# Softplus in one ScalarE instruction, one transposition of dt·x, and eleven to twelve pre-added states in a selective-scan network

## Chip, cores and metric

One core of a Trainium2 chip runs the whole program. The metric is the device time of one execution in microseconds (us); lower is better. Engines are named as the profile names them: PE (TensorE, matmuls), PEld (its weight loads), DVE (VectorE), ACT (ScalarE), POOL (GpSimd) and SP (SyncE, which issues the DMAs).

## The reference

Eight images of 192 channels and 64x64 positions pass through four layers. Layers 0 and 2 hold a selective scan over the 4096 positions in four directions. For each direction, channel and state n of 16:

```python
dt = softplus(einsum('kcr,bkrl->bkcl', dt_proj_w, dts) + dt_proj_b)
h  = h * exp(dt_t[..., None] * A) + (dt_t * x_t)[..., None] * B_t[:, :, None, :]
y  = einsum('bkcn,bkn->bkc', h, C_t)
```

Layer 1 uses a softplus too, but no recurrence: `gain = sum_k(bc * softplus(dtr @ dt_w + dt_b) + D)`, between two layer norms, SiLU gates and 1x1 projections. Layer 3 is a windowed attention-like block made of small convolutions. All is float32.

## The kernel before

**The order of the program.** For each image: `scan_layer` (layer 0), `layer0_out` and `layer1`, `put_sequences`, `scan_layer` again (layer 2), and `between` (the rest of this image together with the start of the next one). So `scan_layer` runs 16 times.

**The scan.** A scan layer has 48 units, `k`. A unit is one pass `d` (forward or backward) over one chunk of 512 positions for one third `v` of the work: v=0 and v=1 are 128 channels of one pair of directions each, v=2 holds the 64 left-over channels of both. The three units v=0, 1, 2 of a chunk follow each other. A unit has eight sub-blocks `j` of 64 positions, and the order of the instructions is written out by hand in one loop over k and j (lines 348 to 398); the scheduler is told to keep it (`tc.manual_schedule()`, line 93). In iteration j each engine gets its part of several units at once, and each engine works through its own queue in order:

- DVE: `scan(k, j)` (lines 286 to 301): two operations of 16 elements that carry the state over (lines 294 and 296), then the scan over 16 states x 64 positions (line 299). At j=2 `finish(k-2)` (line 332 or 336), at j=4 `steps_b(k+2)` (line 220), at j=6 and 7 of v=1 and v=2 the building of the diagonals (line 193).
- PE: `fill(k, j+1)` (line 281) computes the scan's input `u` in PSUM from 32-row slices of the transposed dt·x; `u` has two buffers, so the fill for scan j+1 waits for scan j-1. Then `turn(k+1)` (line 234) at j=2, `steps_a(k+2)` (lines 208 and 210) at j=3, the projection of the next chunk at j=4 and 5 of v=0 (lines 141 to 151), diagonals at j=5 (line 183), and `add_up` (line 324), which sums states over n with an identity matrix.
- ACT: at j=2 the copies of the transposed dt·x out of PSUM (line 236), then the 16 decays `exp(dt·a)` of the next unit (line 244) in groups given by the table DECAY; at j=4 the softplus of unit k+2 (`steps_l`, lines 215 to 217): Abs, Exp and Ln, whose result DVE turns into `max(z,0)+ln(1+exp(-|z|))` (line 220); at j=7 `cut(k+1)` (lines 253 and 254), which saves and clears the first column of the decays.
- POOL: the product with C (line 311), the pre-addition of states 12 to 15 to states 8 to 11 (line 312), and dt·x at j=5 (lines 225 and 226).

Small PSUM results (projection, dt before softplus, transpositions, diagonals) share the tag `misc`, which has two buffers, used in turn.

**Two arrangements.** A fill uses rows (positions) in blocks of 32. `windows()` (line 169) gives two arrangements r=0 and r=1 of the chunk, the second shifted by 64 positions; dt·x is transposed in both (eight transpositions per unit), and is extended by 64 positions for it (line 226).

**Outside the scan.** The other phases are ordered by a list scheduler. An activation function needs its table in ACT; `preload_act_table_set` loads one by hand, and the compiler adds loads where a function is not in the table that is there. In `layer1`, four steps `u` normalise (line 651), make three projections with SiLU (line 657), and then loop four times over the directions with the softplus (lines 670 to 698).

Of the kernel before, what the change touches and what calls it, by code (L numbers as in the profile page):

```python
# [40 lines left out]
def tile_net(ctx: ExitStack, tc: tile.TileContext, a: dict, out: bass.AP):  # L41
# [39 lines left out]
    def scan_layer(pk, wx, wd):  # L81
# [2 lines left out]

        table = tc.keep_in_program_order(nc.scalar.preload_act_table_set(EXP_LN))
        with (
            tc.tile_pool(name="sc_c", bufs=1) as sc,
            tc.tile_pool(name="sc_w", bufs=2) as sw,  # L90
# [11 lines left out]
            nc.sync.dma_start(out=msk, in_=a["msk"])  # L102

            neg_a = sc.tile([P, 3, 2, NS], F32, name="neg_a")
            with tc.issue_after(table.ins):
                nc.scalar.activation(neg_a, par[:, :, :, 0:NS], AF.Exp)
            nc.vector.tensor_scalar_mul(neg_a, neg_a, -1.0)
            skip = sc.tile([P, 3], F32, name="skip")
            nc.vector.tensor_tensor(skip, par[:, :, 0, 17], par[:, :, 1, 17], ALU.add)
# [1 line left out]
            carry = [sc.tile([P, NS], F32, name=f"carry{v}") for v in range(3)]  # L111

            nck = T // Q
            NP = 12
            units = [
                (d, i, i if d == 0 else nck - 1 - i, v)
# [49 lines left out]

            def windows():
                for r in range(2):  # L170
                    for w in range(NSUB // 4):
                        for e in range(2):
                            t0 = r * SB + w * 4 * SB + e
                            yield (r * 2 + w) * 2 + e, slice(t0, t0 + 2 * P - 1, 2)
# [34 lines left out]
                else:  # L209
                    nc.tensor.matmul(pz, wdt[:, d, 1, :], x, start=True, stop=True)  # L210

            def steps_l(k):

                t = dts[k] = sw.tile([P, Q], F32, tag="dt", name="dt")
                nc.scalar.activation(t, pzs[k], AF.Abs)
                nc.scalar.activation(t, t, AF.Exp, scale=-1.0)
                nc.scalar.activation(t, t, AF.Ln, bias=one)  # L217

            def steps_b(k):
                nc.vector.scalar_tensor_tensor(dts[k], pzs.pop(k), 0.0, dts[k], ALU.max, ALU.add)  # L220

            def steps_c(k):
                x = vt[k // 3][:, units[k][3], :]
                dtx[k] = sw.tile([P, Q + SB], F32, tag="dtx", name="dtx")
                nc.gpsimd.tensor_tensor(dtx[k][:, 0:Q], dts[k], x, ALU.mult)  # L225
                nc.gpsimd.tensor_tensor(dtx[k][:, Q : Q + SB], dts[k][:, 0:SB], x[:, 0:SB], ALU.mult)

            def turn(k):

                dtt[k] = sw.tile([P, NSUB, P], F32, tag="dtt", name="dtt")  # L230
                for i, cols in windows():
                    if i % 4 == 0:
                        pt = misc()
                    nc.tensor.transpose(pt[:, i % 4 * P : (i % 4 + 1) * P], dtx[k][:, cols], ident)  # L234
                    if i % 4 == 3:
                        nc.scalar.copy(dtt[k][:, i - 3 : i + 1].rearrange("p i c -> p (i c)"), pt)  # L236

            def decay(k, n0, n1):

# [29 lines left out]
            def fill(k, j):  # L269

                d, i, c, v = units[k]
                s = j if d == 0 else NSUB - 1 - j
                u = us[k, j] = sp.tile([P, NS, SB], F32, tag="u", name="u", bufs=2)
                for e in range(2):
                    for r in range(2):
                        w, q = divmod((s - r) % NSUB, 4)
                        i = (r * 2 + w) * 2 + e
                        rows = slice(q * 32, (q + 1) * 32)
                        for o in ((v,) if v < 2 else (0, 1)):
                            ch = slice(0, P) if v < 2 else slice(o * CB, (o + 1) * CB)  # L280
                            nc.tensor.matmul(  # L281
                                u[ch, r * 8 : r * 8 + 8, e:SB:2], dtt[k][rows, i, ch],
                                dg[k // 3, o][rows, i], start=True, stop=True,
                            )

# [22 lines left out]
            def times_c(k, g):  # L308
                s = 2 * g if units[k][0] == 0 else NSUB - 2 - 2 * g
                h = das[k][:, s : s + 2]  # L310
                nc.gpsimd.tensor_tensor(h, h, cts.pop((k, g)), ALU.mult)  # L311
                nc.gpsimd.tensor_tensor(h[:, :, 8:NP], h[:, :, 8:NP], h[:, :, NP:NS], ALU.add)  # L312

            def load_y(k):
                d, i, c, v = units[k]
# [4 lines left out]
            def add_up(k, n0, n1):  # L320
                if n0 == 0:
                    py[k] = sp.tile([P, Q], F32, tag="py", name="py")
                for n in range(n0, n1):
                    nc.tensor.matmul(  # L324
                        py[k], ident, das[k][:, :, n, :], start=(n == 0), stop=(n == NP - 1)
                    )

            def finish(k):
# [16 lines left out]
            def has(k):  # L345
                return 0 <= k < nu

            for k in range(-6, nu + 2):
                m, v = divmod(k, 3)
                ahead = 0 <= m + 1 < nm  # L350
                for j in range(NSUB):
# [20 lines left out]
                    if j == 2:  # L372
# [3 lines left out]
                            load_y(k - 1)  # L376
                        if has(k + 1):
                            turn(k + 1)
                    if j == 3 and has(k + 2):
                        steps_a(k + 2)  # L380
                    if v == 0 and ahead:
                        if j == 4:
                            project_a(m + 1)
# [7 lines left out]
                    kk = k - 1 if j > 2 else k - 2  # L391
                    if has(kk) and j in SUM:
                        add_up(kk, *SUM[j])
                    if j == 4 and has(k + 2):
                        steps_l(k + 2)
                        steps_b(k + 2)
                    if has(k + 1) and j in DECAY:
                        decay(k + 1, *DECAY[j])

# [222 lines left out]
    def layer1(x):  # L622
        with (
# [25 lines left out]
            with tc.issue_after(table.ins):  # L649
                for u in range(NU):  # L650
                    norm(wk, wide_, part(x, u), vec(0), vec(1), part(xn, u), "sq")
            for u in range(NU):
                src = part(xn, u)
                for dst, ww, c0 in ((s2, w, O_X2), (xs, wc, 0), (z, wc, 192)):
                    ps = linear(psum, ww, c0, src)
                    for i in range(2):
                        nc.scalar.activation(part(dst, u)[i], ps[i], AF.Silu)
            table = tc.keep_in_program_order(nc.scalar.preload_act_table_set(EXP_LN))
            with tc.issue_after(table.ins):
                for u in range(NU):  # L660
                    src, gain = part(xs, u), part(xn, u)
# [8 lines left out]
                    for k in range(4):  # L670
                        pk, pz = wide_("pk"), (wide_("pza"), narrow_("pzb"))
                        r = [slice((k - h) % 4 * 32, (k - h) % 4 * 32 + 32) for h in range(2)]
                        for h in range(2):
                            nc.tensor.matmul(
                                pz[0][:, h], wdt[r[h], h, 0:CA], dtr[r[h], h], start=True, stop=True
                            )
                        for h in range(2):
                            nc.tensor.matmul(
                                pz[1][half(h)], wdt[r[h], h, CA:192], dtr[r[h], h], start=True, stop=True
                            )  # L680
                        for h in range(2):
                            nc.tensor.matmul(
                                pk[:, h], sel[r[h], 0:P], bc[r[h], h], start=True, stop=True
                            )
                        sp_ = step_pair(wk, "sp")
                        for i in range(2):
                            nc.scalar.activation(sp_[i], pz[i], AF.Abs)
                            nc.scalar.activation(sp_[i], sp_[i], AF.Exp, scale=-1.0)
                            nc.scalar.activation(sp_[i], sp_[i], AF.Ln, bias=one)
                            nc.vector.scalar_tensor_tensor(  # L690
                                sp_[i], pz[i], 0.0, sp_[i], ALU.max, ALU.add
                            )
                        if k == 0:
                            spread(tt, gain, sp_, pk, ALU.mult)
                        else:
                            spread(tt, sp_, sp_, pk, ALU.mult)
                            for i in range(2):
                                tt(gain[i], gain[i], sp_[i], ALU.add)
                    for i in range(2):
                        nc.vector.scalar_tensor_tensor(  # L700
                            gain[i], gain[i], d_sum[i], src[i], ALU.add, ALU.mult
                        )
                for u in range(NU):
                    y, s, xc = part(xn, u), part(s2, u), part(x, u)
                    norm(wk, wide_, y, vec(2), vec(3), y, "sq")
# [9 lines left out]
    PE_TAPS = 4  # L715


    def behind(b, pool, wk, psp):

        wide_, narrow_ = psp  # L720
        x = new_pair(pool, "x")
# [24 lines left out]
        yt = [t[:, 0:T] for t in yt]  # L746
        for u in range(NU):
            s = join(narrow_, wk, yt, u)
            norm(
                wk, wide_, s, [v[:, 0:1] for v in v2], [v[:, 1:2] for v in v2], part(x, u), "join"  # L750
            )
            yield "norm"

        xc = room("t2", size["t2"])[:, 0:T]
# [182 lines left out]
            yield "out"  # L937


    def ahead(b, pool, wk, psp):  # L940

        wide_, narrow_ = psp
        w0 = load_both(pool, a["w0"], 384, "w0")
# [21 lines left out]
        yield "load"  # L965
        for u in range(NU):
            hu = part(h, u)
            norm(wk, wide_, hu, col["ln_g"], col["ln_b"], hu, "sta")
            yield "norm"
        for u in range(NU):  # L970
            hu = part(h, u)
# [95 lines left out]
    def between(done, todo):  # L1067

        with (
# [2 lines left out]
            ExitStack() as stack,  # L1072
        ):
            gens = []
            alone = done is None or todo is None
            for name, fn, b in (("c", behind, done), ("a", ahead, todo)):
                if b is None:
# [8 lines left out]
                def narrow_(what, name=name):  # L1086
                    return psp.tile([P, Q], F32, tag="pb" + name, name=what + name, bufs=2)

                gens.append(fn(b, pool, wk, (wide_, narrow_)))
            while gens:  # L1090
                for g in list(gens):
                    if next(g, None) is None:
# [136 lines left out]
```

## Time and profile before

| | |
|---|---|
| three timed runs | 28047.61 us median, 28042.4 to 28049.32 |
| profiled execution | 28045.14 us, span 28043.0 us |
| busy share of the span | PE 85%, DVE 78%, POOL 71%, ACT 49% |
| granted TensorE clock, mean | 0.919 |
| image 0, from the trace: first scan layer | about 209 to 1436 us |
| layer 0's end, layer 1 and the sequences | 1436 to 1948 us (with the second scan layer's start) |
| second scan layer | 1948 to 3177 us |
| `between`, to the next image's first scan | 3177 to 3702 us |
| table loads in the trace | 190, of 1.28 us each |

The profile's page gives the busy time of each engine over the whole span, groups of instructions by source line, and waits by who released them. The timeline lists instructions in order: start, duration, engine, line, operation, and in brackets the idle time ahead of it and who ended it. The windows view gives the busy time of each engine in a stretch and the granted TensorE clock there (1.00 is full speed). Since nearly three quarters of the time lies in sixteen scan layers that repeat one pattern every three units, the place to read is one such chunk.

### The profile page before, as it was taken

The numbers are of one execution on the slowest core, as the hardware profiler recorded it, in microseconds if no ns is written. First come the engines' busy times: TensorE is split into PE (matmuls) and PEld (weight loads), VectorE is DVE, ScalarE is ACT, GpSimd is POOL, SyncE is SP. The second block draws the span as 40 slices with busy tenths as digits, with TensorE's granted clock in tenths as the row PEclk, the third lists the DMA queues.
The fourth block names the chain that finished last, engine by engine and source line by source line (L and its number), as shares of the span: only waits on it lengthen the run. The fifth ranks groups of instructions, "written<-read, shape, count | busy, mean of one in ns | idle before, by whom it ended". The sixth has DMA issues, their size and how long they took to land.

```text
span 28043.0 us, 311528 instructions
## 1 busy us (share of the span) xinstructions
PE 23809.1 (85%) x109960; PEld 10557.4 (38%) x109960; DVE 21950.2 (78%) x25269; ACT 13815.8 (49%) x22366; POOL 19824.5 (71%) x8284
## 2 busy tenths in 40 slices
PE   8979879798797987979889798897988979889797
PEld 3424334243342433424334243342433424334243
DVE  7959779597795977959789597895978859788596
ACT  5545445454454544545445454454544545445453
POOL 6929679296792957929579295792957929579296
PEclk9979989799897998979989799897998979989798
DMA  5626556265562655626556265562655626556264
GB/s 153 193 85 188 145 155 194 83 188 145 157 192 83 190 143 158 193 83 189 142 159 192 83 189 142 160 190 86 191 140 160 187 87 190 141 160 188 88 190 130
DMA packets 1239290, 4286.43 MB, mean 153 GB/s; under 512 B 427920, under 2 KB 454384, under 8 KB 839408
## 3 DMA queue, kind: packets, MB, share of 16 engines
q1 hardware_dynamic: 1237744, 4266.51, 51.7%
q8 instruction: 886, 14.52, 0.2%
q14 instruction: 660, 5.41, 0.1%
HBM read 3810.80 MB, written 450.72 MB: 152 GB/s over the span
## 4 chain that ended last, share of the span: by engine, by line
PE 25%; DVE 23%; ACT 11%; issue 4%; POOL 3%; DMA 2%; SPq 0%; DVEq 0%; POOLq 0%; ACTq 0%
DVE da L299 15%; PE u L281 7%; PE py L324 7%; ACT da L244 5%; PE pa L450 2%; DVE dg L193 1%; DVE u L296 1%; POOL da L311 1%; ACT dtt L236 1%; POOL acc L873 1%; PE misc L234 1%; PE pa L453 1%; ACT dt L217 1%; DVE tmp L294 1%; DVE dt L220 1%
## 5 line engine op out<-in xcount | busy, mean ns | idle before, releaser
L311 POOL TENSOR_TENSOR da<-da,ct 128x2048 f32<-128x2048 f32 x3072 | 13929.5, 4534 | 725.0 <-DVE tmp L294 265.2
L299 DVE TENSOR_TENSOR_SCAN da<-da,u 128x1024 f32<-128x1024 f32 x6144 | 14049.4, 2287 | 379.4 <-ACT da L254 91.5
L324 PE MATMUL py<-da,ident 128*128 128x512 f32 x18432 | 9348.1, 624 | 62.4 <-POOL da L311 62.4
L281 PE MATMUL u<-dg,dtt 32*128 32x256 f32 x65536 | 7075.4, 400 | 1706.2 <-DVE da L299 1677.2
L244 ACT ACTIVATE da<-dt,neg_a 128x512 f32<-128x512 f32 x12288 | 7708.4, 710 | 0.0
L281 PEld LDWEIGHTS u<-dg,dtt 32*128 32x128 f32 x65536 | 4163.9, 161 | 6358.2 <-issue 3972.4
L324 PEld LDWEIGHTS py<-da,ident 128*128 128x128 f32 x18432 | 3137.2, 190 | 4071.7 <-issue 3751.3
L225 POOL TENSOR_TENSOR dtx<-dt,vt 128x512 f32<-128x512 f32 x768 | 978.8, 1275 | 4652.9 <-DMA vt<-vs 3888.5
L312 POOL TENSOR_TENSOR da<-da 128x512 f32<-128x512 f32 x3072 | 3901.7, 1270 | 240.9
L236 ACT COPY dtt<-misc 128x512 f32<-128x512 f32 x1536 | 829.8, 589 | 6277.1 <-PE misc L234 6277.1
L296 DVE TENSOR_TENSOR u<-u,tmp 128x16 f32<-128x16 f32 x6048 | 1106.5, 183 | 703.5 <-PE u L281 55.6
L193 DVE TENSOR_TENSOR dg<-msk,misc 128x1024 f32<-128x1024 f32 x1024 | 1223.1, 1197 | 0.0
L220 DVE SCALAR_TENSOR_TENSOR dt<-misc,dt 128x512 f32<-128x512 f32 x768 | 531.3, 692 | 780.5 <-ACT dt L217 624.4
L234 PE MATMUL misc<-ident,dtx 128*128 128x128 f32 x6144 | 980.6, 304 | 62.2 <-POOL dtx L225 51.4
L294 DVE TENSOR_TENSOR tmp<-da,da 128x16 f32<-128x16 f32 x5376 | 937.9, 174 | 119.0
L234 PEld LDWEIGHTS misc<-ident,dtx 128*128 128x128 f32 x6144 | 818.3, 209 | 342.7 <-issue 225.6
L824 POOL MEMSET t<- 128x4356 f32 (+2 forms) x32 | 99.8, 3120 | 1190.5 <-DVE t L798 1031.0
L858 PE MATMUL pwc<-t,l3taps 128*128 128x486 f32 (+1 forms) x1280 | 724.5, 705 | 241.5 <-DVE u L878 143.5
L253 ACT COPY da<-da 128x128 f32<-128x128 f32 x768 | 294.3, 383 | 1096.9 <-DVE tmp L294 1079.4
L875 DVE SCALAR_TENSOR_TENSOR acc<-t,l3p,acc 128x486 f32<-128x486 f32 (+1 forms) x480 | 479.6, 1026 | 415.0 <-POOL acc L873 411.2
L208 PE MATMUL misc<-xd,wdt 64*128 64x512 f32 x1024 | 615.6, 683 | 13.4 <-ACT xd L155 13.4
L141 PE MATMUL misc<-vt,wxt 128*128 128x512 f32 x512 | 318.0, 706 | 362.9 <-DMA vt<-vs 362.9
(289 smaller groups left out, 19493.8 us busy)
## 6 DMA issues: line engine op xcount, KB each, us to landing
ct<-cd SPq DMA_DIRECT2D x2048, 1024.0 KB
ct<-cd SPq DMA_DIRECT2D x2048, 512.0 KB
vt<-vs SPq DMA_DIRECT2D x768, 256.0 KB
yp<-yo SPq DMA_DIRECT2D x384, 256.0 KB
yo<-yp SPq DMA_DIRECT2D x384, 256.0 KB
ys<-yo SPq DMA_DIRECT2D x384, 256.0 KB
yt<-ys SPq DMA_DIRECT2D x96, 512.0 KB
t<-ys SPq DMA_DIRECT2D x96, 512.0 KB
```

What stands on the lines that cost most here:

```text
L193: nc.vector.tensor_tensor(dg[m, o][:, at], msk[:, 0:32].unsqueeze(1).unsqueeze(1).to_broadcast(shape), bts[m, o][:, at, r * 8 : r * 8 + 8] ...
L225: nc.gpsimd.tensor_tensor(dtx[k][:, 0:Q], dts[k], x, ALU.mult)
L234: nc.tensor.transpose(pt[:, i % 4 * P : (i % 4 + 1) * P], dtx[k][:, cols], ident)
L236: nc.scalar.copy(dtt[k][:, i - 3 : i + 1].rearrange("p i c -> p (i c)"), pt)
L244: nc.scalar.activation(das[k][:, :, n, :], dts[k].rearrange("p (s t) -> p s t", t=SB), AF.Exp, scale=neg_a[:, v, d, n : n + 1],)
L281: nc.tensor.matmul(u[ch, r * 8 : r * 8 + 8, e:SB:2], dtt[k][rows, i, ch], dg[k // 3, o][rows, i], start=True, stop=True,)
L294: nc.vector.tensor_tensor(tmp, da0[:, k % 2, s, :], prev, ALU.mult)
L296: nc.vector.tensor_tensor(head, head, tmp, ALU.add)
L299: nc.vector.tensor_tensor_scan(h, h, u.rearrange("p n t -> p (n t)")[:, way], 0.0, ALU.mult, ALU.add)
L311: nc.gpsimd.tensor_tensor(h, h, cts.pop((k, g)), ALU.mult)
L312: nc.gpsimd.tensor_tensor(h[:, :, 8:NP], h[:, :, 8:NP], h[:, :, NP:NS], ALU.add)
L324: nc.tensor.matmul(py[k], ident, das[k][:, :, n, :], start=(n == 0), stop=(n == NP - 1))
```

## The change

1. **Softplus.** In the scan the three ACT instructions and the DVE one become one ACT instruction `Softplus`. Its table does not hold Exp, so the three units of the next chunk are done together, in v=1 at j=3 and j=4, between two table loads; `dt` gets four buffers. In layer 1 the same replacement is made, and the table loads there are placed by hand: norms, SiLU, softplus and the last norms each under one load. In `between` the norms are placed behind one load.
2. **One transposition.** dt·x is transposed once (four transpositions instead of eight). The first arrangement is one ACT copy of the PSUM tile; the second is made by four more ACT copies of 32 partitions x 512 elements each, shifted by 32 partitions. The extension by 64 positions on POOL goes.
3. **Pre-added states.** POOL adds four states for the first two of a unit's four groups, and three for the last two; the state left out is summed by one more PE matmul over half the columns.

```diff
-            def steps_l(k):
-                t = dts[k] = sw.tile([P, Q], F32, tag="dt", name="dt")
-                nc.scalar.activation(t, pzs[k], AF.Abs)
-                nc.scalar.activation(t, t, AF.Exp, scale=-1.0)
-                nc.scalar.activation(t, t, AF.Ln, bias=one)
             def steps_b(k):
-                nc.vector.scalar_tensor_tensor(dts[k], pzs.pop(k), 0.0, dts[k], ALU.max, ALU.add)
+                dts[k] = sw.tile([P, Q], F32, tag="dt", name="dt", bufs=4)
+                nc.scalar.activation(dts[k], pzs.pop(k), AF.Softplus)
             def steps_c(k):
-                dtx[k] = sw.tile([P, Q + SB], F32, tag="dtx", name="dtx")
-                nc.gpsimd.tensor_tensor(dtx[k][:, 0:Q], dts[k], x, ALU.mult)
-                nc.gpsimd.tensor_tensor(dtx[k][:, Q : Q + SB], dts[k][:, 0:SB], x[:, 0:SB], ALU.mult)
+                dtx[k] = sw.tile([P, Q], F32, tag="dtx", name="dtx")
+                nc.gpsimd.tensor_tensor(dtx[k], dts[k], vt[k // 3][:, units[k][3], :], ALU.mult)
             def turn(k):
-                for i, cols in windows():
-                    if i % 4 == 0:
-                        pt = misc()
-                    nc.tensor.transpose(pt[:, i % 4 * P : (i % 4 + 1) * P], dtx[k][:, cols], ident)
-                    if i % 4 == 3:
-                        nc.scalar.copy(dtt[k][:, i - 3 : i + 1].rearrange("p i c -> p (i c)"), pt)
+                pt = misc()
+                for i, cols in windows(1):
+                    nc.tensor.transpose(pt[:, i * P : (i + 1) * P], dtx[k][:, cols], ident)
+                pt = pt.rearrange("p (w x) -> p w x", w=2)
+                nc.scalar.copy(dtt[k][:, 0], pt)
+                for q in range(4):
+                    src = pt[(q + 1) % 4 * 32 : (q + 1) % 4 * 32 + 32]
+                    nc.scalar.copy(dtt[k][q * 32 : q * 32 + 32, 1], src if q < 3 else src[:, ::-1])
             def times_c(k, g):
-                nc.gpsimd.tensor_tensor(h[:, :, 8:NP], h[:, :, 8:NP], h[:, :, NP:NS], ALU.add)
+                n = NS - NP if g < 2 else NS - NP - 1
+                to = h[:, :, NP - n : NP]
+                nc.gpsimd.tensor_tensor(to, to, h[:, :, NS - n : NS], ALU.add)
             def add_up(k, n0, n1):
+                if n0 < NP // 2 <= n1:
+                    s = slice(0, NSUB // 2) if units[k][0] else slice(NSUB // 2, NSUB)
+                    nc.tensor.matmul(py[k][:, s.start * SB : s.stop * SB], ident,
+                        das[k][:, s, NP, :], start=False, stop=False)
...
-                    if j == 3 and has(k + 2):
-                        steps_a(k + 2)
+                    if v == 1 and ahead:
+                        if j == 3:
+                            steps_a(k + 2)
+                            steps_a(k + 3)
+                        if j == 4:
+                            steps_b(k + 2)
+                            steps_a(k + 4)
+                            steps_b(k + 3)
+                            steps_b(k + 4)
-                    if j == 4 and has(k + 2):
-                        steps_l(k + 2)
-                        steps_b(k + 2)
...
+            table = tc.keep_in_program_order(nc.scalar.preload_act_table_set("silu_and_others"))
+            with tc.issue_after(table.ins):
                 (three projections with SiLU)
-            table = tc.keep_in_program_order(nc.scalar.preload_act_table_set(EXP_LN))
+            table = tc.keep_in_program_order(nc.scalar.preload_act_table_set("softplus"))
-                            nc.scalar.activation(sp_[i], pz[i], AF.Abs)
-                            nc.scalar.activation(sp_[i], sp_[i], AF.Exp, scale=-1.0)
-                            nc.scalar.activation(sp_[i], sp_[i], AF.Ln, bias=one)
-                            nc.vector.scalar_tensor_tensor(sp_[i], pz[i], 0.0, sp_[i], ALU.max, ALU.add)
+                            nc.scalar.activation(sp_[i], pz[i], AF.Softplus)
```

## The prediction

> **What bounds the kernel now.** I read first the windows view, to see which engine sets the pace in a scan layer (the second row is the whole first scan layer), then the three timelines of one unit, then the groups.
>
> ```profile
> core 0: us, PE busy (x) PEld busy (x) DVE busy (x) ACT busy (x) POOL busy (x), PEclk, DMA share, GB/s
> 209.00:1436.00 1227.00, 1127.23 (x6000) 544.89 (x6001) 1126.60 (x1292) 658.83 (x1152) 1171.77 (x474) 0.98 0.62 187
> ```
>
> 1227 us are 48 units of 25.6 us, or 16 chunks of 76.7. PE, DVE and POOL are each busy over 90% of it and the clock is nearly full: three engines run abreast. What ends each step is seen on DVE, in a unit v=1 whose first scan starts at 776.39:
>
> ```profile
> 788.19 2.29 DVE L299 TENSOR_TENSOR_SCAN da<-da,u 128x1024 f32<-128x1024 f32 x1
> 791.25 0.69 DVE L220 SCALAR_TENSOR_TENSOR dt<-misc,dt 128x512 f32<-128x512 f32 x1 [0.77 <-ACT dt L217]
> ...
> 792.35 2.29 DVE L299 TENSOR_TENSOR_SCAN da<-da,u 128x1024 f32<-128x1024 f32 x1
> ...
> 795.16 2.29 DVE L299 TENSOR_TENSOR_SCAN da<-da,u 128x1024 f32<-128x1024 f32 x1
> ```
>
> Scan to scan is 2.81 us where only the two small operations lie between, and 4.16 where L220 does. So DVE is the chain, and L220 costs 1.34 here: its own time plus 0.77 of waiting for ACT's Ln. Over all scan layers the median unit is 24.27, 26.49 and 26.05 us for v=0, 1, 2, a chunk 76.81; L220 adds 0.94, 1.34 and 0.90 to them, 3.18 per chunk. Next, what ACT and PE do in that unit:
>
> ```profile
> 783.88 1.07 ACT L236 COPY dtt<-misc 128x512 f32<-128x512 f32 x2 [7.63 <-PE misc L234]
> 784.85 4.40 ACT L244 ACTIVATE da<-dt,neg_a 128x512 f32<-128x512 f32 x7
> 789.15 0.58 ACT L215 ACTIVATE dt<-misc 128x512 f32<-128x512 f32 x1
> ```
>
> ```profile
> 784.47 1.13 PE L281 MATMUL u<-dg,dtt 32*128 32x256 f32 x8
> 785.53 1.12 PE L208 MATMUL misc<-xd,wdt 64*128 64x512 f32 x2
> 786.58 1.98 PE L324 MATMUL py<-da,ident 128*128 128x512 f32 x4
> 788.50 1.13 PE L281 MATMUL u<-dg,dtt 32*128 32x256 f32 x8
> 789.56 1.98 PE L324 MATMUL py<-da,ident 128*128 128x512 f32 x4
> ```
>
> ACT works through seven decays before the softplus; PE reaches its second fill of this piece 12.1 us after the unit's first scan (788.50) and has no idle time on the way.
>
> **Part 1, softplus in the scan.** It removes L220 from DVE: 256 chunks x 3.18 = 814 us, if nothing else came late. It removes three ACT instructions (0.58 + 0.63 + 0.72) per unit and adds one; the trace has no Softplus, and I take Abs's 0.58, the simplest row of that shape (bounds 0.48, the spacing of the copies, and 1.93, the three it replaces). It adds two table loads per chunk, each 1.28:
>
> ```profile
> L493 ACT ACT_TABLE_LOAD x35 | 44.9, 1283 | 89.7 <-PE pa L453 74.5 <-PE paa L453 15.0
> ...
> L1061 ACT COPY ev<-pcola 64x512 f32<-64x512 f32 x64 | 37.2, 581 | 30.7 <-PE pcola L1055 21.8 <-DMA vs<-ev 7.9
> ```
>
> ACT as a whole has room (659 of 1227 us), so total work is no problem; the order is. In v=1, j=4, PE's queue reads: fill 5, `steps_a(k+4)`, two states of `add_up`, fill 6. `misc` has two buffers, and `steps_a(k+2)` and `(k+3)` hold both. So `steps_a(k+4)` waits until Softplus(k+2) has read its buffer; behind it in PE's queue stand the sums and fill 6, and for fill 6 DVE waits with scan 6.
>
> *When ACT gets there*, from the unit's first scan: copies start at +7.5 before (783.88 - 776.39); with half the transpositions and the later arrival of the PE I take about +7.4. Then five copies at 0.485 (2.43), seven decays at 0.63 (4.35; they stand ahead of the softplus in ACT's queue), the load 1.28, Softplus 0.58, and some 0.4 of hand-overs: +16.5. *When PE gets there*: before, fill 5 ends at +13.2; half a turn less (-0.6), one `steps_a` more (+0.9) and the wait of `steps_a(k+3)` for the copies (+0.9) make +14.4. PE idles 2.1. Then `steps_a` 1.05, two states x two halves 1.92, fill 1.06: fill 6 ends at 20.5, scan 6 starts at 20.9 instead of 17.44 had nothing waited. The stall is 3.45 us, against 1.34 saved in the same unit.
>
> Units after the change: v=1 26.49 - 1.34 + 3.45 = 28.6; v=2 26.05 - 0.90 = 25.15; v=0 only 23.96 rather than 23.33, because the projection, its copy out and the next unit's work on ACT and PE then end last (projection's end at +17.5, +0.15, then 6.31 to the next first scan). The chunk is 77.7, +0.9. The second load, in front of the nine decays left, delays them by 1.28; ACT has over 7 us idle before each unit's copies (the bracket at L236), which hides it. Without that cover it would cost 1.28 per chunk.
>
> **Part 2, one transposition.** PE loses 4 of 8 transposes (1.22 to about 0.65 us) per unit, ACT gains 3 copies net. The trace has no copy of 32 partitions; L1061 shows that half the partitions (64) take 581 ns like a full one, so I take the full price, 0.485 spacing (bounds: 0.12 if time went by partitions, 0.59 if nothing overlapped, -1.5 to +0.4 on the wait above). POOL loses the small extension, about 0.3 of 24.2 us per unit, and one state in two of four groups, together 0.9; POOL had 1.1 us idle per unit, so this gives nothing by itself.
>
> **The clock.** Here removal of PE work can cost. In the trace, the granted clock changes in steps of 3.41 us. I weighed each matmul record by the share of the array's rows and columns it uses and its length (uninterrupted 128x128 by 512 columns is 1). All some 4,900 scan windows of weight 0.42 or more were followed by full clock; seven of weight 0.35 to 0.41 were each followed by half clock. One of them:
>
> ```profile
> 2608.38:2611.79 3.41, 2.75 (x18) 1.92 (x17) 3.13 (x5) 3.41 (x6) 3.33 (x4) 1.00 1.16 405
> 2611.79:2615.21 3.42, 3.42 (x8) 1.26 (x6) 3.32 (x4) 0.99 (x3) 3.42 (x2) 0.51 0.95 206
> ```
>
> The first is busy for 2.75 of 3.41 us, the second is at 0.51. The lightest window of a normal unit lies at the turn (v=0 and v=2) and weighs 0.422, hardly above the edge. Half a turn less takes 0.48/3.41 = 0.14 off: in v=0 windows that start from +4.15 to +6.3 fall to 0.28 to 0.39. These are 2.15 of 3.41 us of starting phases, 63%. A half-clock window loses up to 1.7 us; in v=0 light windows follow each other and PE's projection is on the path to the next unit, so I take two windows less 0.55 of slack (PE's usual idle ahead of such a fill), 2.85: 63% x 2.85 = 1.8. In v=1 PE's 2.1 us gap makes 74% of phases light at 1.65, 1.2; in v=2 18% at about 1, 0.2. Together 3.15 per chunk. The bounds are 0 and about 5 (every phase, every window).
>
> "TensorE: Matmul & The Clock Gate", section on the HAM clock gate, of the Trainium skill says that the clock falls back after at least one idle window of about 3.4 us. By that rule a gap of 2.1 us would not drop it and this term would be 0; the seven drops, with PE busy 2.75 of 3.41 us, speak for a threshold on work. "ScalarE: Activation LUTs", section "What ACT_TABLE_LOAD costs", puts a drain of about 1.38 us on each switch; in this trace the load at 28.13 begins as the activation before it ends and the next starts 1.29 later, so no drain shows. By the page the stall would be some 1.4 longer, an estimated +330 us.
>
> **Part 3, pre-added states.** One more half matmul (about 0.24 us) per unit on PE at j=6, ahead of fill 7; with the turn halved PE still has less to do. Bounds 0 to 0.25 per unit; I take 0.
>
> **Layer 1.** In the loop over directions (four steps of 30.4 us per image) PE waits 2.5 us per step for the softplus chain and its DVE end. With one instruction instead of four, three steps give 2.4 each, the last gives its four dropped ACT operations and DVE's (4.2), the first 2: 13 us per image, 104 in all (bounds 16 and 200). The loads placed by hand keep norms from overlapping the projections but drop some loads: -4 to +6 per image, taken as 0. One more load ahead of each scan layer's first units: 16 x 1.28 = 20.
>
> **Sum**, against the profiled execution's 28045 us: 240 chunks with a following one x (0.9 + 3.15 = 4.05) = +972; the 16 last chunks of a layer have no softplus to do, 16 x -3 = -48; layer 1 -104; loads +20. That is 28,885; the median of the timed runs is 2.5 above the profiled one: **28,890 us**, 3% slower.
>
> **Rivals.**
> 1. *Stall, and the clock holds.* The edge at 0.41 rests on seven events. Then a chunk is +0.9: 240 x 0.9 - 48 - 104 + 20 = +84, **28,130** (27,770 if the copies take their lower bound and the wait is 1.5 shorter, 28,450 if Softplus takes its upper one). For it: PE is still over 80% busy in every light window.
> 2. *Faster: ACT is in time.* If Softplus(k+2) ends by +14.4, PE never waits, and the chunk keeps the gain of L220 as far as v=0's other path lets it: 0.31 + 1.34 + 0.90 = 2.55. 240 x -2.55 - 48 - 104 + 20 = -744, **27,300**. It needs 2.1 us off the 9 between the copies' start and Softplus's end, and full clock. For it: a copy of 32 partitions at its lower bound gives 1.5. Against: L1061, and decays that are fixed by their row.
> 3. *The replacement does not need its loads* (a table with both functions): excluded by the changed program's order, which has 632 loads against 190.
>
> **Chances.** Stall with clock drops 0.60 (28,400 to 29,350); stall alone 0.24, of which 0.05 lies below and 0.05 within 0.2%; ACT in time 0.12, and 0.04 for faster still. Measurement tells 0.2% (56 us) from no change. So faster 0.05 + 0.12 + 0.04 = 0.21, same 0.05, slower 0.74. The range leaves out the two fast cases and the heaviest clock losses: 27,750 to 29,200.
>
> **What would show it.** Right: PE idle some 2 us ahead of `steps_a` in v=1, put down to ACT's softplus; a scan step in v=1 at j=6 of about 6 us; steps at j=4 of 2.82; a mean granted clock in the scan below 0.9. Wrong: j=6 of v=1 at 2.8 to 3.8 us; copies of 32 partitions much under 0.5; clock at 0.98 as before; v=0 units shorter than 23.9.

## The result, and the profile after

The changed kernel takes 28,692.06 us (median; 28,689.33 to 28,695.35) beside 28,045.01 for the kernel before on the same chip: a ratio of 1.0232, with a 95% interval of 1.0214 to 1.0250. It is slower, as forecast, by 647 us where 842 were forecast. The profiled execution has a span of 28,693.6 us against 28,043.0, so 650.6 us are to be found. From the two traces, cut at the first and last scan of each layer (sixteen scan layers; a chunk is three units):

| stretch | before | after | difference, us | forecast |
|---|---|---|---|---|
| 240 chunks with a following one, mean of one | 77.18 | 81.04 | 240 x 3.865 = +928 | 240 x 4.05 = +972 |
| 16 last chunks of a layer, mean of one | 69.93 | 68.74 | -19 | -48 |
| eight stretches from first to second scan layer | 4123.8 | 3882.0 | -242 | -104; +20 for loads over this row and the next |
| `between`, start and end | 4278.0 | 4261.8 | -16 | see above |

Per chunk, the means of the units moved by +0.80 (v=0), +3.80 (v=1) and -0.73 (v=2). The first scan layer in the windows view, with the columns shown earlier:

```profile
195.70:1482.50 1286.80, 1202.88 (x5907) 562.96 (x5908) 1099.14 (x1246) 730.21 (x1229) 1133.55 (x428) 0.92 0.58 178
```

DVE is busy 27 us less, since L220 is gone, and PE 76 us more, although the turn was halved: the granted clock is 0.92 instead of 0.98, so the same matmuls take longer. Over the 240 chunks the trace has 14.0 us at half clock per chunk, 3.2 before. Some 46 us lie in the first chunk of a layer in both kernels; for each of the other 224 chunks it is 11.7 us against 0.1. Now a unit v=1 whose first scan starts at 793.76, on DVE:

```profile
805.55 2.29 DVE L296 TENSOR_TENSOR_SCAN da<-da,u 128x1024 f32<-128x1024 f32 x1
807.87 0.18 DVE L291 TENSOR_TENSOR tmp<-da,da 128x16 f32<-128x16 f32 x1
812.39 0.18 DVE L293 TENSOR_TENSOR u<-u,tmp 128x16 f32<-128x16 f32 x1 [4.34 <-PE u L278]
812.61 2.29 DVE L296 TENSOR_TENSOR_SCAN da<-da,u 128x1024 f32<-128x1024 f32 x1
...
817.61 0.18 DVE L293 TENSOR_TENSOR u<-u,tmp 128x16 f32<-128x16 f32 x1 [2.50 <-PE misc L183]
817.83 2.29 DVE L296 TENSOR_TENSOR_SCAN da<-da,u 128x1024 f32<-128x1024 f32 x1
```

L220 is gone, and in its place DVE waits 4.34 us for fill 5 and 2.50 for fill 6 (PE's last instruction before the second release is a diagonal, which is why L183 is named). What PE did meanwhile:

```profile
802.89 1.12 PE L208 MATMUL misc<-xd,wdt 64*128 64x512 f32 x2
804.68 1.94 PE L208 MATMUL misc<-xd,wdt 64*128 64x512 f32 x2 [0.67 <-ACT dtt L231]
806.56 3.78 PE L323 MATMUL py<-da,ident 128*128 128x512 f32 x4
810.27 2.08 PE L278 MATMUL u<-dg,dtt 32*128 32x256 f32 x8
812.28 2.08 PE L210 MATMUL misc<-xd,wdt 128*128 128x512 f32 x2
```

From the second line on every duration is nearly twice what it was (3.78 for four matmuls that took 1.98). In these lines PE stands still only once, 0.67 us, at `steps_a(k+3)`, for the copies of the turn. At `steps_a(k+4)`, the last line, there is no wait. ACT:

```profile
802.29 2.34 ACT L231 COPY dtt<-misc 32x512 f32<-32x512 f32 x4
804.66 4.40 ACT L241 ACTIVATE da<-dt,neg_a 128x512 f32<-128x512 f32 x7
809.07 1.28 ACT L214 ACT_TABLE_LOAD   x1
810.37 1.09 ACT L214 ACTIVATE dt<-misc 128x512 f32<-128x512 f32 x2
```

Softplus(k+2) ends at about +17.2 from the unit's first scan (forecast: +16.5), but the slow PE arrives at +18.5 (forecast: +14.4). And the two windows of the clock:

```profile
801.44:804.85 3.41, 2.56 (x13) 1.24 (x13) 3.27 (x5) 3.09 (x6) 3.33 (x2) 1.00 0.04 10
804.85:808.26 3.41, 3.41 (x4) 1.04 (x5) 2.99 (x5) 3.41 (x6) 3.26 (x2) 0.50 0.97 300
```

The light window is the one with the halved turn (0.74 us), a fill of 32 rows, a dt matmul of 64 rows and the 0.67 us gap; the next runs at 0.50.

### The profile page after: what moved, and what is told of

Its sections match the earlier page's. It is cut to its first block, busy times and chain, and to the rows that moved or that the text cites. A ratio compares the mean times of both kernels' runs of the same rounds, so it can differ in the third digit from the quotient of the medians.

```text
span 28693.6 us, 306665 instructions
## 1 busy us (share of the span) xinstructions
PE 24736.5 (86%) x108424; PEld 10774.2 (38%) x108424; DVE 21263.7 (74%) x24245; ACT 14515.5 (51%) x23064; POOL 19194.1 (67%) x7516
## 4 chain that ended last, share of the span: by engine, by line
PE 28%; DVE 24%; ACT 5%; issue 4%; POOL 3%; DMA 2%; SPq 0%; DVEq 0%; POOLq 0%; ACTq 0%
DVE da L296 16%; PE py L323 11%; PE u L278 7%; DVE dg L193 2%; PE pa L460 2%; POOL da L308 2%; ACT da L241 1%; DVE u L293 1%; ACT dtt L231 1%; POOL acc L883 1%; DVE tmp L291 1%; PE misc L210 1%; PE pa L463 1%; PE misc L208 1%; PE misc L141 1%
## 5 line engine op out<-in xcount | busy, mean ns | idle before, releaser
L323 PE MATMUL py<-da,ident 128*128 128x512 f32 x18432 | 10158.9, 672 | 54.4 <-POOL da L308 54.4
L278 PE MATMUL u<-dg,dtt 32*128 32x256 f32 x65536 | 7305.0, 410 | 1216.8 <-DVE da L296 1205.8
L323 PEld LDWEIGHTS py<-da,ident 128*128 128x128 f32 x18432 | 3408.9, 206 | 4486.5 <-issue 4306.5
L228 ACT COPY dtt<-misc 128x512 f32<-128x512 f32 x768 | 450.2, 586 | 6337.0 <-PE misc L226 6337.0
L311 POOL TENSOR_TENSOR da<-da 128x512 f32<-128x512 f32 (+1 forms) x3072 | 3478.0, 1132 | 240.9
L231 ACT COPY dtt<-misc 32x512 f32<-32x512 f32 x3072 | 1771.9, 577 | 46.1
L208 PE MATMUL misc<-xd,wdt 64*128 64x512 f32 x1024 | 707.2, 824 | 161.4 <-ACT dtt L231 148.0
L214 ACT ACTIVATE dt<-misc 128x512 f32<-128x512 f32 x768 | 430.8, 595 | 464.1 <-PE misc L210 453.8
L155 ACT ACTIVATE xd<-misc,msk 128x512 f32<-128x512 f32 x256 | 175.9, 687 | 886.9 <-PE misc L151 886.9
L460 PE MATMUL pa<-sqa,mean_w 128*128 128x512 f32 x384 | 313.8, 965 | 336.8 <-ACT sqa L500 336.8
```

Source lines behind the costliest of these rows:

```text
L208: nc.tensor.matmul(pz, wdt[r, d, 0, :], x[r], start=True, stop=True)
L231: nc.scalar.copy(dtt[k][q * 32 : q * 32 + 32, 1], src if q < 3 else src[:, ::-1])
L278: nc.tensor.matmul(u[ch, r * 8 : r * 8 + 8, e:SB:2], dtt[k][rows, r, w, e * P + ch.start : e * P + ch.stop], dg[k // 3, o][rows, i], start ...
L311: nc.gpsimd.tensor_tensor(to, to, h[:, :, NS - n : NS], ALU.add)
L323: nc.tensor.matmul(py[k], ident, das[k][:, :, n, :], start=(n == 0), stop=(n == NP - 1))
```

## Experiments

*Theory:* the halved turn makes single clock windows too light, so PE falls to half clock, and besides, PE's queue waits in v=1 for ACT. *Rival:* the wait for ACT is the whole loss, and the low clock only goes along with it. Times are medians; ratios are against runs of the kernel before on the same chip. The kernel before has medians between 28,032 and 28,045 on these chips, so a difference in microseconds between two runs can carry some 13 us of that. "Chunk" is the mean over the 240 chunks. A unit has a drop when a window at half clock begins in it; drops are counted over the 224 units of each v away from a layer's ends.

**1. The turn's PE work put back** (`twice`):

```diff
-                for i, cols in windows(1):
-                    nc.tensor.transpose(pt[...], dtx[k][:, cols], ident)
+                for _ in range(2):
+                    for i, cols in windows(1):
+                        nc.tensor.transpose(pt[...], dtx[k][:, cols], ident)
```

> The changed kernel with each of the four transpositions of a unit issued twice into the same place, so that PE has its old amount of work at the turn and nothing else moves; the output is unchanged. Theory (half the turn's PE work gone lets the clock fall; behind that stands PE's wait for Softplus): v=0 units go from a mean of 25.3 us to 23.7 with no half-clock window left, v=2 stays near 25.1, v=1 keeps the wait and one half-clock window after it, 30.8; a chunk 79.6 instead of 81.0, the kernel about 28,350 us. Rival (the wait for Softplus is the whole loss and the low clock only goes along with it): the extra transposes are extra work, the kernel stays at 28,690 or gets slower by up to 768 x 0.6 = 460 us.

28,166 us (1.0050, 1.0035 to 1.0065): 526 us faster than the changed kernel, by adding useless work, and 184 us less than expected. The chunk is 78.98. v=0 has no drop left in 224 units (187 in the changed kernel) and takes 23.84; v=2 25.11; v=1 30.03, of which 49 units have no drop. In one of these (first scan at 850.18, 29.07 us long) the forecast's wait stands without the clock, beside a wait of 0.91 us for the copies at `steps_a(k+3)`:

```profile
864.59 1.13 PE L279 MATMUL u<-dg,dtt 32*128 32x256 f32 x8
867.96 1.12 PE L210 MATMUL misc<-xd,wdt 128*128 128x512 f32 x2 [2.23 <-ACT dt L214]
```

Fill 5 ends, and `steps_a(k+4)` waits 2.23 us for Softplus. The rival's "no gain" is out for v=0; for v=1 both costs are there.

**2. Softplus ahead of the decays of j=3** (`early`), and **3. both edits** (`early_twice`):

```diff
                         if j == 3:
                             steps_a(k + 2)
+                            steps_b(k + 2)
                             steps_a(k + 3)
                         if j == 4:
-                            steps_b(k + 2)
                             steps_a(k + 4)
...
+            LATE = {2: (0, 3), 4: (3, 9), 5: (9, 12), 6: (12, 16)}
```

In v=1 the table LATE stands in place of DECAY.

> The changed kernel with its softplus put ahead of the decays of j=3 on ACT (three decays, load, three Softplus, load, thirteen decays), so that the third dt matmul finds its buffer free; the turn stays halved. Theory: the clock still falls at about +11 in v=1 and at +8 in v=0; the slowed PE hides most of the wait anyway, so removing the wait alone gives little: v=1 29.5 to 30.5 instead of 30.5, v=0 unchanged at 25.3, the kernel 28,450 to 28,690 us. Rival (the wait is the whole loss): v=1 falls to about 26.5, v=0 to 24, the kernel to about 27,400 us.

> Both edits: transpositions issued twice, and softplus ahead of the decays of j=3. Theory: neither the clock nor the wait costs any more; v=0 23.7, v=1 25.5 to 26.5 (ACT's own work, from the copies at +7.4 to the cut, is 18.4 us and then ends last), v=2 25.1; a chunk 74.3 to 75.3, the kernel 27,080 to 27,320 us: the two together gain far more than the sum of each alone. Rival (only the wait): as with the softplus moved alone, 27,400 us or some 100 to 400 us more for the extra transposes.

`early` gives 28,710 us (1.0243, 1.0227 to 1.0258), no gain at all and 20 us above what the theory allowed; 208 of 224 units v=1 drop, at 31.0 us, and the 16 without a drop take 27.14. So the wait alone was not what cost. `early_twice` gives 27,976 us (0.9980, 0.9971 to 0.9990): 716 us faster than the changed kernel, and more than the two edits' sum (526 - 18), but 656 us above the upper edge of what I expected. v=1 is 29.16, where 25.5 to 26.5 was expected: 172 units still drop, and without a drop they take 27.6. PE still waits for the five copies before `steps_a(k+3)`:

```profile
627.78 1.12 PE L208 MATMUL misc<-xd,wdt 64*128 64x512 f32 x2 [0.91 <-ACT dtt L232]
```

In each of the 172 units the light window ahead of the drop holds this wait (median weight 0.33). The expectation overlooked this third wait.

**4. The old transposition** (`twoarr`: `turn`, `steps_c` and the index in `fill` as before the change; Softplus and pre-addition as after).

> The changed kernel with the old transposition put back (eight transposes, two copies, and the extension of dt x input); Softplus, its order and the pre-added states stay. Theory: the turn's PE work is back, so no clock loss in v=0; ACT has 1.75 us less to copy ahead of Softplus, so the wait shrinks from 2.1 us to some 0.5: v=0 23.7, v=1 26, v=2 25.1, a chunk 74.8, the kernel about 27,200 us. Rival (the wait alone): the wait shrinks by 1.75 us of 3.8 lost in v=1, v=0 and the clock as in the changed kernel, about 28,270 us.

27,685 us (0.9875, 0.9858 to 0.9891), 485 us above the expected 27,200, and a chunk of 76.94. v=0 and v=2 as expected (23.84, 25.11, no drop); v=1 27.99 instead of 26. The wait did not shrink to 0.5:

```profile
463.41 1.13 PE L275 MATMUL u<-dg,dtt 32*128 32x256 f32 x8
466.33 1.12 PE L210 MATMUL misc<-xd,wdt 128*128 128x512 f32 x2 [1.78 <-ACT dt L214]
```

ACT is done with Softplus(k+2) 2.0 us sooner (+15.2 from the first scan at 451.07), but PE too is there sooner (+13.5), as nothing holds it at `steps_a(k+3)`; 1.78 us remain, and in 113 of 224 units a window that holds them is followed by a drop.

**5. No wait left** (`split`: the old transposition, and the three softplus at two places):

```diff
                     if v == 1 and ahead:
                         if j == 3:
                             steps_a(k + 2)
-                            steps_a(k + 3)
                         if j == 4:
                             steps_b(k + 2)
-                            steps_a(k + 4)
-                            steps_b(k + 3)
-                            steps_b(k + 4)
+                    if v == 2 and ahead and j < 2:
+                        steps_a(k + 2 + j)
+                        steps_b(k + 2 + j)
```

> The changed kernel with the old transposition (eight transposes, two copies) and the three Softplus of a chunk split over two places: the first as it is, in v=1 at j=3 and 4, the other two in v=2 at j=0 and 1, where ACT and PE wait for the scan anyway; four table loads per chunk instead of two. Theory (PE's waits at the dt matmuls, and the clock that falls behind them, are the loss): PE waits for no softplus, no clock is lost, v=0 23.7, v=1 25.2, v=2 25.1 to 26; a chunk 74 to 75, the kernel 26,990 to 27,230 us. Rival (table loads themselves are what costs): two more of them, 240 x 2.6 = 620 us more than with the old transposition alone, about 28,300 us.

27,066 us (0.9654, 0.9638 to 0.9670): the fastest version, faster than both kernels, with twice the table loads in the scan. The chunk is 74.33; no unit of the 672 has a drop (what is left of half clock lies in the first chunk of each layer, 43.7 us there). Its first scan layer:

```profile
198.30:1384.00 1185.70, 1141.76 (x6095) 556.83 (x6096) 1098.91 (x1246) 681.68 (x1118) 1146.76 (x475) 0.98 0.63 193
```

DVE has the same 1099 us of work as in the changed kernel, in 101 us less time. With two loads more per chunk than `twoarr` it is 619 us faster: the loads themselves are not what cost, but what waits behind them.

**6. The clock alone** (`split_one`: `split` with the single transposition).

> The split softplus (one in v=1, two in v=2, four loads per chunk) with the single transposition and its five copies, so that the halved turn is the only thing left of the loss and PE waits for no softplus. Theory: the clock falls at the light turns and costs by itself, since PE is busy all the time behind them: 1.3 us per half-clock window that DVE has to wait for, v=0 25.3, v=1 26 to 27, v=2 25.3, a chunk 76.5 to 77.5, the kernel 27,590 to 27,830 us. Rival (a low clock costs nothing where no wait stands behind it): as with the old transposition, 27,070 us within 60.

27,599 us (0.9843, 0.9829 to 0.9856), 533 more than `split`. The chunk is 76.29, +1.96, nearly all of it in v=0 (23.84 to 25.79): 23.73 without a drop (19 units, as in `split`, so the five copies themselves cost nothing there), 25.07 with one half-clock window (124), 26.65 with two (41), 28.35 with three (40). v=1 and v=2 stay at 25.38 and 25.12: v=1 has no drop, v=2 has 24, which cost nothing that can be seen. The two dt matmuls now stand at the start of v=2, in its light stretch, and PE waits for no softplus in v=1. The low clock costs by itself, but in v=0 alone, where I had expected it in v=1 too.

**7 and 8. The same amount of work elsewhere** (`heavy` in `add_up`, `late` in `fill`):

```diff
+                if n0 == 0:
+                    nc.tensor.matmul(py[k][:, 0 : Q // 2], ident, das[k][:, 0 : NSUB // 2, 0, :], start=True, stop=True)
...
+                if j == 7:
+                    flat = u.rearrange("p n t -> p (n t)")
+                    for i in range(4):
+                        nc.tensor.transpose(flat[:, i * P : (i + 1) * P], ident, ident)
```

> The changed kernel with one extra half matmul per unit (128x128 by 256 columns) at the start of each sum over states, at j=3, as much PE work as the four doubled transposes but behind the light stretch; the result is overwritten by the matmul after it, so the output is unchanged. Theory (the clock is decided by the work inside single windows of 3.41 us): the light windows stay, about 14 us at half clock per chunk as in the changed kernel, 28,690 to 28,900 us. Rival (any PE work added lifts the clock): as with the transposes doubled, about 28,170 us.

> The changed kernel with four extra 128x128 transpositions per unit, just as many as were doubled at the turn, but issued ahead of fill 7 at j=6, 10 us or more behind the light stretch; they write into the buffer that fill 7 overwrites, so the output is unchanged. Theory (single windows of 3.41 us decide over the clock): the light windows stay as in the changed kernel, half-clock windows in 60 to 90% of the v=0 units and 11 to 15 us per chunk, and the kernel gets no faster: 28,600 to 29,100 us. Rival (any added PE work lifts the clock): as with the transposes doubled at the turn, no drop in v=0, about 28,170 us.

28,497 us (1.0161, 1.0146 to 1.0176) and 28,521 us (1.0169, 1.0152 to 1.0186). Both miss their lower edge, by 193 and 79 us, and lie far above the rival's 28,170; the half clock is 9.8 and 10.5 us per chunk, also less than expected (about 14, and 11 to 15). v=0 keeps drops in 121 and 123 of 224 units, against 0 with the same work at the turn: the place decides. But it was 187 in the changed kernel. Part of it may be where the chunks fall against the clock's windows: before, the first window boundary after a unit's start is spread evenly (28 to 39 units v=0 in each seventh of a window); in the changed kernel 107 of 224 fall in one seventh, its commonest chunk (82.0 us) being 24.02 windows long. An edit that changes the chunk's length shifts that. Why the two fell by just so much isn't settled; for `heavy` the extra matmul (j=3) may also reach into the latest of the light windows.

**9. One transposition on the kernel before** (`oneturn`).

> The kernel before with the one transposition alone (four transposes, five copies, no extension of dt x input); Abs, Exp, Ln and DVE's addition stay. Theory: two costs. The copies last 1.3 us longer net of the shorter turn, so Ln comes later and DVE waits for it at j=4 in all three units, 3.9 us per chunk; and the halved turn drops the clock in v=0 and v=2, another 1.3 to 3 us per chunk: 76.8 becomes 82 to 84, the kernel 29,280 to 29,750 us with 7 us or more at half clock per chunk. Rival (the clock falls only where PE waits for a buffer as well): 3.9 per chunk and a clock as before, about 28,970 us.

29,528 us (1.0528, 1.0513 to 1.0544), the chunk 83.18 (+6.00): the time is as expected, the split of it is not. DVE's wait ahead of L220, in the groups of the kernel before and of this one:

```profile
L220 DVE SCALAR_TENSOR_TENSOR dt<-misc,dt 128x512 f32<-128x512 f32 x768 | 531.3, 692 | 780.5 <-ACT dt L217 624.4 <-issue 97.2 <-DMA vt<-vs 58.1
```

```profile
L220 DVE SCALAR_TENSOR_TENSOR dt<-misc,dt 128x512 f32<-128x512 f32 x768 | 531.1, 692 | 2305.4 <-ACT dt L217 2093.3 <-issue 95.2 <-POOL da L315 51.4
```

It grew by 1525 us, 1.99 per unit, which is 5.96 of the 6.00 per chunk. The halved turn does not bring the copies forward: they start at +7.10 in v=0 in both kernels, for in the old one the first copy waits only for the first four transposes. And they end 1.87 later (10.04 against 8.17). The clock was low for 15.9 us per chunk, more than in the changed kernel, and cost little (v=0: 25.96 without a drop, 26.0 and 26.6 with a first one at +9 and +8; what stands out are the units that begin at half clock, 30 of v=2 with 30.5 against 28.0, and five each of v=0 and v=1): DVE waits for ACT there whatever PE does.

**10. Pre-added states on the kernel before** (`preadd`).

> The kernel before with the change of the pre-added states alone (POOL adds three instead of four states in the last two groups of a unit, PE sums the state left out with one more half matmul). Theory: DVE sets the pace, so POOL's 0.55 us less per unit and PE's 0.25 us more are both hidden: 27,985 to 28,095 us. Rival: the half matmul stands ahead of fill 7 on a PE that has no idle time there, 0.25 us per unit, 768 x 0.25 = 190, about 28,230 us.

28,164 us (1.0045, 1.0031 to 1.0059): slower, the rival's way, but between the two (28,095 at most, or about 28,230). In a unit v=1 (first scan at 710.79) and the unit v=0 before it, PE, ACT and DVE:

```profile
708.28 0.59 PE L331 MATMUL py<-da,ident 128*128 128x256 f32 x2
708.80 1.13 PE L281 MATMUL u<-dg,dtt 32*128 32x256 f32 x8
...
717.94 1.22 PE L234 MATMUL misc<-ident,dtx 128*128 128x128 f32 x8
```

```profile
718.72 1.07 ACT L236 COPY dtt<-misc 128x512 f32<-128x512 f32 x2 [7.96 <-PE misc L234]
```

```profile
726.08 0.69 DVE L220 SCALAR_TENSOR_TENSOR dt<-misc,dt 128x512 f32<-128x512 f32 x1 [1.20 <-ACT dt L217]
```

In the kernel before, the turn of the unit that starts at 776.39:

```profile
783.10 1.22 PE L234 MATMUL misc<-ident,dtx 128*128 128x128 f32 x8
```

The half matmul in v=0 (two records; the fill behind it starts 0.52 us after its start) makes the PE, which has no idle time until the turn of v=1, start that turn 0.43 later (medians: +7.15 instead of +6.72); copies, Ln and L220 follow, and DVE waits 1.20 instead of 0.77. By this v=1 is 0.40 longer, 95 of the 151 us that the 240 chunks lose; v=2 adds 35 (27 of its 224 units now drop and take 27.3 instead of 26.0) and v=0 21.

**11. The best version without part 3** (`split_nopre`).

> The split softplus with the old transposition, and the pre-addition as before the change (four states in every group, no half matmul). POOL's rows then add up to 4 x 4.53 + 4 x 1.27 + 1.60 = 24.8 us per unit, 74.4 per chunk, where the split version's chunk takes 74.3. Theory (POOL is next behind DVE): the chunk becomes 74.7 to 75.2, the kernel 27,150 to 27,270 us, so the pre-addition that did nothing for the kernel before is worth 100 to 200 us here. Rival (the half matmul on PE costs as much as POOL gains): 27,070 us within 40.

27,222 us (0.9710, 0.9696 to 0.9723): 156 more than `split`, so there the lighter POOL pays. But the chunk is only 74.57, below what I expected; from the traces, 58 of the 163 us are in the 240 chunks, some 40 in the 16 last ones and the rest between the layers. That POOL sets a step inside the chunk is not shown.

**12. Layer 1 alone** (`layer1`: the kernel before with `layer1` and everything after it in the file from the changed kernel).

> The kernel before with the change of layer 1 and of the norms' table loads alone (one Softplus there, loads placed by hand); the scan is as before. From the traces, the stretches between a first and a second scan layer fell by 242 us and the start by 13 in the changed kernel. Theory: this part stands by itself and none of it comes from the scan's end or start: about 27,790 us, all of the gain in those stretches. Rival (the forecast's 104 us are right and the rest comes from the scan's shorter ends): about 27,930 us.

27,759 us (0.9895, 0.9881 to 0.9910): 281 us gained. The stretches between first and second scan layers sum to 3858.6 against 4123.8, 265 us less; 24 more are in `between`, start and end. The gain stands alone. The loop over directions of image 0, in the kernel before and in this one, by windows:

```profile
1649.00:1768.50 119.50, 110.39 (x259) 29.32 (x259) 94.62 (x108) 82.24 (x102) 0.00 (x0) 0.67 0.00 0
```

```profile
1645.00:1735.00 90.00, 80.54 (x259) 23.57 (x258) 76.77 (x87) 33.34 (x39) 0.00 (x0) 0.90 0.00 1
```

ACT falls from 82 to 33 us, and the same 259 matmul records take 81 us of PE instead of 110, at a clock of 0.90 instead of 0.67. PE's idle time is 9.1 and 9.5 us in these windows, so the 29.5 us show as shorter matmuls. Why the clock rises with the shorter chain isn't shown.

## Why the prediction was right, and where its steps failed

- **The direction and the chunk** held: +3.86 per chunk, forecast 4.05. That they agree so closely is partly luck: with their shares of the clock, v=0 was forecast at 25.76 and took 25.29, v=1 at 29.8 and took 30.46, v=2 at 25.35 and took 25.30. (The three clock terms add up to 3.2, not 3.15: 12 us in all.) Of L220's 3.18 us, v=0 and v=2 kept what was said: their steps at j=4 are 2.82, and units without a drop take 23.72 and 25.10 (forecast 23.96 and 25.15).
- **The order of events in v=1 failed.** The text had PE waiting 2.1 us at `steps_a(k+4)` and the clock falling in that gap, with the long step at j=6. In most units the clock falls first, at +10 to +12, in the window of the halved turn and the short wait of `steps_a(k+3)`, and the long steps are those from scan 4 to 5 (5.1 to 7.0 us in nine of ten) and 5 to 6 (3.8 to 5.5). Slowed, PE arrives after Softplus. The forecast wait is there where the clock holds until then: 35 of 224 units, which take 30.8 us, and in `twice` the 49 units without a drop: there the step to scan 6 takes 6.14 us, as forecast, but the step to scan 5 takes 3.98, which the forecast had at 2.82, and the unit 29.6 instead of 28.6. The two costs hide each other, which is why removing the wait alone (`early`) gave nothing.
- **The clock's threshold was right, the forecast's frequencies too low.** v=0 drops in 187 of 224 units (83%, forecast 63%, which took all phases as equally likely); a drop costs 1.34 us with one window and 2.9 with two (`split_one`), where 2.85 was taken each time, and most have one. So v=0 lost 1.6 us by the clock where 1.8 was forecast: more drops, each cheaper. v=1: all 224 (forecast 74%). v=2: 57 of 224 (25%, forecast 18%). The sign named for it, a mean clock below 0.9 in the scan, did not come (0.92 in the first layer).
- **ACT's prices.** Softplus took 0.595 us (taken: Abs's 0.58). A copy of 32 partitions takes 577 ns, and four follow each other in 2.34 us, 0.59 apart: not 0.485, let alone a quarter. The copies of v=1 start at +7.93, not +7.4; 0.43 of that is the half matmul's (`preadd`). So Softplus ended 0.7 us later than said, though the hand-overs were shorter.
- **Part 3 was costed at nothing, "PE still has less to do".** The half matmul holds PE for 0.52 us and not 0.24. The part costs 123 us alone, most of it through the later turn of v=1, and gains 156 in `split` against `split_nopre`, where nothing else is late.
- **Layer 1 was mis-sized**: 104 us forecast, 242 in the changed kernel and 265 in `layer1`. The step counted PE's waits of 2.5 us per u, and not that PE ran at 0.67 of its clock there. The clock, which the forecast weighed for the scan, was left out where it was low already.
- **The last chunks** gave 1.2 us and not 3. That isn't looked into.
- **Rivals.** "The clock holds" is wrong by the trace. "ACT in time" did not happen in the changed kernel, but `split` shows that its gain was there to be had, and more: 2.85 us per chunk below the kernel before. The rival asked for 2.1 us less ahead of Softplus; what gave the gain was another order (in `split_one`, with all five copies, v=1 takes 25.38 too). The third rival stayed excluded: the trace has 632 loads.
- "TensorE: Matmul & The Clock Gate", section on the HAM clock gate, of the Trainium skill speaks of an idle window; here the windows of the scan that were followed by half clock had PE busy in 70% of their time (median of all fourteen traces). "ScalarE: Activation LUTs", section "What ACT_TABLE_LOAD costs", names a drain beside the load; here the load at 809.07 starts 0.01 us after the last decay ends and Softplus, at 810.37, 0.02 us after the load ends, so that only the 1.28 us show.

## What to carry to other kernels

Before taking work off an engine with a granted clock, weigh its lightest windows: PE work that looks free to remove may be what keeps the rest at full speed, and useless work in the right place can be worth more than the saving. When several uses of one table are gathered to save loads, look at whose queue then waits for the whole group; two more loads at a place where the engine idles were cheaper than one wait. And after a stall is found, remove it together with its neighbours: one cost behind another shows nothing when taken away alone.

## What the runs showed of the hardware

Over the scan layers of all fourteen traces, each window of 3.41 us at full clock that lies between a layer's first and last scan was weighed by the matmul records in it (rows x columns of the array used, times elements; 1.0 for back-to-back 128x128 by 512 at 0.48 us). Of 3,099 windows below 0.40, all but one were followed by half clock; of 69,759 from 0.43 up, three were. In between it goes either way, from 80% at 0.40 to 2% at 0.42. Time busy does not part them so: of 6,146 windows in which PE was busy for 70 to 80% of the time, 1,788 were followed by half clock. In these traces, then, the threshold is on work done by the array and not on time busy, and a matmul of 32 rows counts a quarter of one of 128: with rows left out of the weight the best threshold is wrong in 2,655 of 73,863 windows, with them in 116. A copy by ACT of 32 partitions costs as much as one of 128 (577 and 586 ns).
